# A graph convolution on one core: in steps 0 to 3, a chunk's message is made ahead of the last sum of a later pair's softplus on VectorE

## The chip, the core and the metric

The kernel runs on one core of one Trainium2 chip. Its time is the device time of one execution in microseconds (us), and of several runs the median. Engines are named as in the profile: PE (TensorE, matmuls), PEld (its weight loads), DVE (VectorE), ACT (ScalarE), POOL (GpSimd) and SP (SyncE, which here only issues DMAs). Each engine goes through its own queue in order; they wait for each other through semaphores.

## What is computed

A layer of a SchNet-like graph network with a residual: 12500 nodes with 128 features, 412500 directed edges with 20 radial features and a weight each. Shortened from the reference:

```python
h = jnp.maximum(_layernorm(x, axis=-1), 0.0)
def ssp(x): return jax.nn.softplus(x) - LOG2
h = h @ W_in2f
Wij = ssp(f_ij @ W_f1 + b_f1) @ W_f2 + b_f2      # per edge, 128 filters
Wij = Wij * rcut_ij[:, None]
x_ij = h[idx_j] * Wij                            # idx_j = dst (sorted)
agg = jax.ops.segment_sum(x_ij, idx_i, num_segments=N)   # idx_i = src
return x + ssp(agg @ W_o1 + b_o1) @ W_o2 + b_o2
```

## The kernel before

Edges are taken in order, in 806 chunks of 512 (four tiles of 128 edges); four chunks make a group, which shares its input loads. A chunk goes through these parts, each a method of `Group`:

- `rows` (L608): SP fetches the 32 rows of h near the chunk's destinations into `near`, as three bf16 parts. `window` (L744): DVE compares the destinations, relative to the chunk's first (`rel`, loaded by SP at L593), with row numbers, which gives a selection matrix `at`.
- `hidden`, `hidden_log`, `hidden_end`, for a pair of chunks together (1024 edges): PE makes z = f W_f1 (L653) in a PSUM buffer of which there is one; ACT takes the absolute value and the exponential (L656, L657), then the logarithm (L662); DVE adds the rest of the softplus, r = max(z, -b) + a (L668). That is "the last sum of a pair's softplus".
- `bias` (L753 for chunks 0 and 1, else L757 on ACT) puts the second bias into a PSUM buffer v; `value` (L764) adds r W_f2 to it on PE; `pick` (L772) selects h's rows with `at` and `near` on PE, and `picked` (L780) scales them by the edge weight on ACT into `hg`, in four instructions.
- `message` (L789, L791, L795): for the first chunk of a pair DVE copies the places of its edges into `o`; then DVE multiplies v by hg into `o`, and POOL scatters the four tiles to `slots`, a table in DRAM, each row to a slot of its own near the other edges of its source node.
- `blocks`, `rank`, `rank_end` (L673, L692, L725, L697, L717 to L721) count the free slots: DVE marks the sources' blocks, PE adds the marks up in one PSUM buffer `free`, and DVE reduces and makes the slots' numbers.

The table has seven segments; when a segment's chunks are through, its units are loaded by SP (L833), compared (L844) and added up by matmuls (L857), beside the chunks of the segments after it. Clears of the tables go out on SP (L1099) by a plan of due times. After the last chunk the last segment is added up and the output part is made.

The order of work is written out by hand. `step(k)` runs for k from -1 on, and each call puts instructions on the queues of all engines, for several chunks at different depths: `part(name, upto, make)` makes a part for all chunks that are due and not made yet. The part "end" is made up to chunk min(k + 2, the last one with a logarithm), and `pairs` lets it do something only for the first chunk of a pair; so it does something in steps of even k. The part "window" is made up to k + 2, and at k = 0 up to 1. The message of a step is that of chunk k; its value and pick are those of chunk k + 1, and its bias that of chunk k + 2. The buffers that matter: three for `r`, three for `at`, four for `o`, two for `hg`, three in PSUM for v and the picked rows together, one for z.

In the first steps normalisation and projection of h (`make_h`) stand between the parts, a piece after each step.

Of the kernel before, what the change touches and what calls it, by code (L numbers as in the profile page):

```python
# [41 lines left out]
def gnn_kernel(  # L42
# [475 lines left out]
    with tc.tile_pool(name="edge", bufs=2) as edge, tc.tile_pool(  # L518
# [367 lines left out]
        LG, LW, LR, LZ = 12, 6, 6, 4  # L886

        def of(k):
            return groups[k // NCHUNK], k % NCHUNK
# [6 lines left out]
        made = {}  # L896

        def part(name, upto, make):

            for j in range(made.get(name, -1) + 1, min(upto, NCH - 1) + 1):  # L900
                make(*of(j))
                made[name] = j

        def pairs(make):
            return lambda g, c: None if c % 2 else make(g, c)
# [22 lines left out]
        def group(j):  # L928
            if j not in groups and j < NG:
                groups[j] = Group(j)  # L930

        def ranks(j):

            if 0 <= j < NCH:
                g, c = of(j)
                g.rank(c)
                yield
                g.rank_end(c)

        def step(k, units=()):  # L940

            def has(j):
                return 0 <= j < NCH

            group((k + LG) // NCHUNK)
            part("rows", min(k + LW, 2 * k + 3, NEXT if k < NEXT - 3 else NCH), rows)
            for c, u in units:
                c.load(u + AHEAD)  # L950

            part("blocks", min(k + LR + 1, 2 * k + 1), blocks)
            part("end", min(k + LZ - 2, made.get("log", -1)), pairs(hidden_end))
            part("window", k + 2 if k > 0 else k + 1, window)
            if has(k):
                g, c = of(k)
                g.message(c, vs.pop(k), hgs.pop(k))
            for c in owed:
                c.keep()
            owed.clear()  # L960
            if has(k + 1):
                g, c = of(k + 1)
                vs[k + 1] = g.value(c, bs.pop(k + 1))
                ps = psum.tile([P, QT, P], F32, name="picked", tag="v", bufs=3)
                g.pick(c, ats.pop(k + 1), ps)
            if has(k + 2):

                bs[k + 2] = of(k + 2)[0].bias(of(k + 2)[1])
            if has(k + 1):
                hgs[k + 1] = g.picked(c, ps)  # L970
            for c, u in units:
                c.compare(u)
            upto = max(made["rank"], min(k + LR, 2 * k + 1))
            ready = [ranks(j) for j in range(made["rank"] + 1, upto + 1)]
            made["rank"] = upto
            for r in ready[:1]:
                next(r, None)
            part("hidden", k + LZ, pairs(hidden))
            part("log", k + LZ - 1, pairs(hidden_log))
            for c, u in units:  # L980
                if summed:
                    summed[0].add(summed[1])
                summed[:] = c, u
            for r in ready:
                for _ in r:
                    pass
# [21 lines left out]
        end = NCH + 6  # L1008
        rate = {}
        while len(rate) < len(at):  # L1010
# [4 lines left out]
            end = at[j]  # L1015
# [9 lines left out]
        i, k = 0, todo[0][0]  # L1025
# [43 lines left out]
        with tc.manual_schedule():  # L1069
# [27 lines left out]
            for k in range(-1, max(NCH, max(units) + 1)):  # L1097
                for seg, d in zeros.get(k, ()):
                    seg.clears.append(nc.sync.dma_start(*d).ins.name)  # L1099
                now = units.get(k, ())  # L1100
                for c, u in now:
                    if u == 0:
                        for i in range(AHEAD):
                            c.load(i)
                step(k, now)

                for m in h:
                    next(m, None)
                if k > NEXT - 3:
                    next(aside, None)  # L1110
# [101 lines left out]
```

## Time and profile before

| what | value |
|---|---|
| median of three runs | 5770.01 us (5732.79, 5770.01, 5771.6) |
| the profiled execution, own time | 5772.48 us |
| its span, first to last instruction | 5770.8 us |
| mean granted TensorE clock | 0.718 |
| busy: PE, PEld, DVE, ACT, POOL | 3877.3, 2912.2, 3382.9, 2715.3, 3103.5 us |
| scatters of POOL (L795) | 3224, of 962 ns each |
| sums of the softplus on DVE (L668) | 403, of 1281 ns each |
| products on DVE (L791) | 806, of 680 ns each |
| first scatter starts | 29.44 us |

In the profile's groups a row reads: line, engine, operation, tile written <- tiles read, shapes, count | busy us, mean ns of one | idle time of the engine just before them and what ended it. In the timeline a row begins with start and duration in us, and the bracket at its end is the idle time ahead of it and its releaser. "remote" is an event that the profile puts down to none of the core's engines; "issue" means that nothing that the profile shows was waited for.

### The profile page before, as it was taken

What the parts mean: (1) busy time and instruction counts of PE and PEld (TensorE: products, weight loads), DVE (VectorE), ACT (ScalarE), POOL (GpSimd) and SP (SyncE); (2) the same over time, 40 slices, a digit from 0 to 9 for tenths busy, and PEclk for the clock granted to TensorE, in tenths of its full rate; (3) what the DMA queues carried; (4) which work ended last, traced back from release to release, by engine and by line L of the source; (5) the groups of instructions that cost most, each with busy time, mean ns of one, the idle gap of its engine ahead of it and who ended that gap; (6) DMA issues with size and microseconds to landing.
All of it is one profiled execution on the core that took longest, in us unless ns stands there. A gap on an engine that the chain in (4) does not pass through costs nothing. (4 is left out here: it accounts for less than half of the span.)

```text
span 5770.8 us, 71871 instructions
## 1 busy us (share of the span) xinstructions
PE 3877.3 (67%) x21576; PEld 2912.2 (50%) x21576; DVE 3382.9 (59%) x6726; ACT 2715.3 (47%) x5490; POOL 3103.5 (54%) x3244
## 2 busy tenths in 40 slices
PE   5556555556555555577777777777777777777778
PEld 3333333333333333356655666566566665655557
DVE  5555555555444444466665666666666666566767
ACT  4455554555444444444444444444444444444444
POOL 5555555555555555555555555555555555555550
PEclk7665566565556566578777787788877788787879
DMA  5444443343333333255664554655555555555547
GB/s 150 138 135 141 130 141 119 115 137 104 99 89 87 106 109 87 82 152 161 188 183 137 158 160 144 190 163 157 160 168 173 154 150 178 165 141 153 145 126 215
DMA packets 515581, 820.80 MB, mean 142 GB/s; under 512 B 177074, under 2 KB 312870, under 8 KB 515186
## 3 DMA queue, kind: packets, MB, share of 16 engines
q1 hardware_dynamic: 411586, 602.85, 37.4%
q0 software_dynamic: 103168, 213.15, 11.2%
q8 instruction: 176, 2.88, 0.2%
q14 instruction: 219, 1.79, 0.1%
q10 hardware_dynamic: 432, 0.13, 0.0%
HBM read 419.09 MB, written 396.64 MB: 141 GB/s over the span
## 5 line engine op out<-in xcount | busy, mean ns | idle before, releaser
L795 POOL DMA_INDIRECT slots<-o,slot x3224 | 3100.3, 962 | 2522.6 <-DVE o L791 1605.2
L764 PE MATMUL v<-wf,r 128*128 128x128 f32 x6448 | 1209.4, 345 | 527.4 <-ACT a L657 207.3
L857 PEld LDWEIGHTS acc<-to,m 128*128 128x128 f32 x8132 | 1249.1, 238 | 577.1 <-issue 280.8
L857 PE MATMUL acc<-to,m 128*128 128x128 f32 x8132 | 1342.0, 329 | 271.0 <-DVE agg L880 136.4
L764 PEld LDWEIGHTS v<-wf,r 128*128 128x128 f32 x6448 | 1077.6, 251 | 850.7 <-issue 301.8
L780 ACT ACTIVATE hg<-picked,rcut 128x128 f32<-128x128 f32 x3224 | 913.1, 365 | 1256.6 <-remote 801.2
L697 DVE TENSOR_REDUCE top<-free 128x4 f32<-128x392 f32 x806 | 451.5, 560 | 1650.5 <-remote 990.2
L757 ACT ACTIVATE v<-bf 128x512 f32<-128x512 f32 x804 | 478.0, 595 | 1212.9 <-DVE o L791 888.5
L653 PE MATMUL z<-f,wf 20*128 20x512 f32 x1612 | 661.1, 881 | 406.9 <-DVE r L668 242.4
L844 DVE TENSOR_TENSOR to<-count_ps,m 128x512 f32<-128x512 f32 (+3 forms) x824 | 644.7, 806 | 255.3 <-remote 109.3
L772 PE MATMUL picked<-near,at 96*128 96x128 bf16 x3224 | 398.5, 257 | 495.3 <-ACT hg L780 317.4
L668 DVE SCALAR_TENSOR_TENSOR r<-z,nbf,a 128x1024 f32<-128x1024 f32 x403 | 516.2, 1281 | 242.3 <-ACT a L662 136.3
L656 ACT ACTIVATE a<-z,bf 128x1024 f32<-128x1024 f32 x403 | 454.0, 1127 | 400.4 <-remote 267.8
L772 PEld LDWEIGHTS <-at 96*128 96x128 bf16 x3224 | 315.5, 118 | 558.1 <-issue 531.3
L791 DVE TENSOR_TENSOR o<-v,hg 128x512 f32<-128x512 f32 x806 | 547.8, 680 | 16.8 <-ACT hg L780 12.8
L744 DVE TENSOR_TENSOR at<-count_ps,rel 96x512 bf16<-96x512 f32 x806 | 545.3, 677 | 0.0
L653 PEld LDWEIGHTS z<-f,wf 20*128 20x128 f32 x1612 | 174.6, 241 | 620.9 <-issue 428.9
L662 ACT ACTIVATE a<-a,half 128x1024 f32<-128x1024 f32 x403 | 468.1, 1162 | 0.0
L673 DVE TENSOR_TENSOR inb<-count_ps,blk 128x392 f16<-128x392 f32 x806 | 445.9, 554 | 0.0
L657 ACT ACTIVATE a<-a 128x1024 f32<-128x1024 f32 x403 | 425.8, 1057 | 12.8
L725 PE MATMUL free<-inb,rest_of 128*128 128x392 f16 x806 | 335.3, 416 | 117.6 <-issue 46.9
L692 PE MATMUL free<-inb,after 128*128 128x392 f16 x806 | 335.9, 417 | 17.4 <-issue 13.6
(108 smaller groups left out, 1142.5 us busy)
## 6 DMA issues: line engine op xcount, KB each, us to landing
m<-slots SPq DMA_DIRECT2D x311, 387.0 KB
m<-slots SPq DMA_DIRECT2D x317, 258.0 KB
rel<-rel_d SPq DMA_DIRECT2D x202, 384.0 KB
m<-slots SPq DMA_DIRECT2D x172, 322.5 KB
slots<-o,slot POOLq DMA_INDIRECT x3224
slots<-zero SPq DMA_DIRECT2D x96, 387.0 KB
slots<-zero SPq DMA_DIRECT2D x64, 516.0 KB
f<-in_f_t SPq DMA_DIRECT2D x404, 80.0 KB
```

Source lines behind the costliest of these rows:

```text
L653: nc.tensor.matmul(z[:, k, :], wf1[rows, :], self.f[rows, :], start=True, stop=True)
L662: nc.scalar.activation(a, a, AF.Ln, bias=half, scale=0.5)
L668: nc.vector.scalar_tensor_tensor(r, z, nbf1, a, op0=ALU.max, op1=ALU.add)
L744: nc.vector.tensor_tensor(at, prow_ps.to_broadcast([WP, CH]), self.rel[:, c, :], op=ALU.is_equal)
L757: nc.scalar.activation(v, spread(bf12, QT), AF.Copy)
L764: nc.tensor.matmul(v[:, i, :], r[:, i * P:(i + 1) * P], wf2, start=False, stop=True, skip_group_check=True)
L772: nc.tensor.matmul(ps[:, i, :], at[:, i * P:(i + 1) * P], near, start=i == 0, stop=i == QT - 1, skip_group_check=True)
L780: nc.scalar.activation(hg[:, i, :], ps[:, i, :], AF.Copy, scale=self.rcut[:, j:j + 1])
L791: nc.vector.tensor_mul(o[:, :, :P], v, hg)
L795: put = nc.gpsimd.indirect_dma_start(out=views[j % VIEWS], out_offset=bass.IndirectOffsetOnAxis(ap=self.slot[:, j:j + 1], axis=0), in_=o[: ...
L844: nc.vector.tensor_tensor(to[:, :n, :], count_ps[:, None, :].to_broadcast([P, n, P]), self.m[u][:, :n, P:].to_broadcast([P, n, P]), op=ALU ...
L857: nc.tensor.matmul(self.acc[b // QT][:, i, :], m[:, j, :P], to[:, j, :], start=t == 0, stop=t == self.seg.tiles(b) - 1)
```

## The change

In steps with k < 4 the part "end" is made after the message of the step, and not ahead of the part "window"; from step 4 on the order is as before.

```diff
             part("blocks", min(k + LR + 1, 2 * k + 1), blocks)
-            part("end", min(k + LZ - 2, made.get("log", -1)), pairs(hidden_end))
+            early_on = k < 4
+
+            def end():
+                part("end", min(k + LZ - 2, made.get("log", -1)), pairs(hidden_end))
+
+            if not early_on:
+                end()
             part("window", k + 2 if k > 0 else k + 1, window)
             if has(k):
                 g, c = of(k)
                 g.message(c, vs.pop(k), hgs.pop(k))
+            if early_on:
+                end()
             for c in owed:
                 c.keep()
```

## The prediction

> **What bounds the kernel now.** I read the page first, for the span and the load of each engine, then the view of waits for the whole span, then the timeline of the first 60 us, since the edit acts only there.
>
> The page:
>
> ```profile
> span 5770.8 us, 71871 instructions
> PE 3877.3 (67%) x21576; PEld 2912.2 (50%) x21576; DVE 3382.9 (59%) x6726; ACT 2715.3 (47%) x5490; POOL 3103.5 (54%) x3244
> L795 POOL DMA_INDIRECT slots<-o,slot x3224 | 3100.3, 962 | 2522.6 <-DVE o L791 1605.2
> ```
>
> No engine is full: PE, the busiest, is busy for 67%. The kernel is a pipeline whose steps wait for one another: 806 messages of four scatters each (3224), and POOL, which sends them, idles 2522.6 us, mostly for DVE's product (L791).
>
> The view of waits:
>
> ```profile
> POOL slots L795 <- DVE o L791: 1605.2, 358, 25.4
> DVE top L697 <- remote: 990.2, 163, 12.1
> ACT v L757 <- DVE o L791: 888.5, 325, 9.0
> ```
>
> The columns are us in total, times, and the longest. DVE stops longest at the reduction L697, which needs the ranking matmuls; those stand on PE behind the matmuls that need the rows of `near` fetched by SP. ACT refills a PSUM buffer (L757) only when L791 has read it. So a step is a ring DVE - ACT - PE - DVE with DMA arrivals in it. What the edit can win for good is a shift of this ring at the start; nothing makes a later step shorter.
>
> The timeline, DVE alone, around steps 0 and 2 (start, duration, instruction, idle time before it and its releaser):
>
> ```profile
> 19.61 0.53 DVE L673 TENSOR_TENSOR inb<-count_ps,blk 128x392 f16<-128x392 f32 x1
> 26.60 1.28 DVE L668 SCALAR_TENSOR_TENSOR r<-z,nbf,a 128x1024 f32<-128x1024 f32 x1 [6.46 <-ACT a L662]
> 27.80 0.68 DVE L744 TENSOR_TENSOR at<-count_ps,rel 96x512 bf16<-96x512 f32 x1
> 28.47 0.68 DVE L791 TENSOR_TENSOR o<-v,hg 128x512 f32<-128x512 f32 x1
> 29.83 0.57 DVE L697 TENSOR_REDUCE top<-free 128x4 f32<-128x392 f32 x1 [0.68 <-PE free L692]
> ...
> 39.07 1.27 DVE L668 SCALAR_TENSOR_TENSOR r<-z,nbf,a 128x1024 f32<-128x1024 f32 x1
> 40.26 0.68 DVE L744 TENSOR_TENSOR at<-count_ps,rel 96x512 bf16<-96x512 f32 x1
> 40.86 0.16 DVE L789 COPY o<-place 128x8 f32<-128x8 f32 x1
> 40.93 0.68 DVE L791 TENSOR_TENSOR o<-v,hg 128x512 f32<-128x512 f32 x1
> 41.53 0.55 DVE L697 TENSOR_REDUCE top<-free 128x4 f32<-128x392 f32 x1
> ```
>
> In step 0, DVE stands idle for 6.46 us at the sum L668 (pair 2, 3), until ACT's logarithm ends, with message 0 behind it. In step 2 the same sum (pair 4, 5) waits for nothing: DVE goes through it back to back.
>
> PE, and the DMA engines while this happens (timeline, then the table by stretches, whose last columns are granted clock, DMA share, GB/s):
>
> ```profile
> 28.54 0.61 PE L772 MATMUL picked<-near,at 96*128 96x128 bf16 x4 [3.45 <-DVE at L744]
> 34.28 0.61 PE L772 MATMUL picked<-near,at 96*128 96x128 bf16 x4 [0.47 <-issue]
> 40.58 1.46 PE L653 MATMUL z<-f,wf 20*128 20x512 f32 x4
> ```
> ```profile
> 25.00:29.00 4.00, 0.55 (x6) 0.47 (x6) 2.40 (x4) 1.93 (x4) 0.00 (x0) 1.00 1.02 312
> ```
>
> The pick of chunk 1 waited for `at`, which stood behind the sum. In 25 to 29 us the DMA engines have no room (share 1.02, 312 GB/s).
>
> **The change, part by part.** It adds no work. It moves one part past another in steps 0 to 3, but the sum is made only for the first chunk of a pair and a fixed distance ahead, so in steps 1 and 3 there is none to move. Two places change, all on DVE's queue: steps 0 and 2. There `at`, the copy of places and the product come ahead of the sum. The orders of PE, ACT, POOL and SP stay; what they wait for comes at other times.
>
> Step 0. `at` needs only `rel`, so it follows L673 at 20.1 us instead of 27.80. The product then needs ACT's L780 for chunk 0 (four, started 21.10, 1.14 us in all, so 22.24): it runs at about 22.3 instead of 28.47, 6.2 us earlier. POOL starts 0.97 us after the product starts (28.47 to 29.44), so the first scatter goes at about 23.2 instead of 29.44. Behind the product now waits the sum, but it had to wait for ACT until 26.57 anyway; the cover is 26.6 - 22.9 = 3.7 us, and the sum keeps its 26.60.
>
> What is late next. After the sum DVE reaches L697 at 27.8 instead of 29.83, if the ranking matmuls are done: PE's pick of chunk 1 can follow the values that end at about 25.1 (started 23.01, 2.08 us), so yes. DVE leads by 29.83 - 27.80 = 2.0 us through step 1. PE has one buffer for z: L653 for pair 4, started 29.73 before, now waits for the sum's end at 27.9, about 1.6 to 1.8 us earlier. Then the pick of chunk 2 needs its `near`. The 256-byte packets, which these fetches alone use, ran for chunks 2 and 3 from 30.31 to 32.6 us in the trace, landing at 32.9. The pick stood at 34.28, so its lead can be at most 34.28 - 32.95 = 1.33 us. And message 0's four scatters, 4 x 128 rows x 516 B = 264 KB, started packets at 31.16 and now start them some 6 us sooner, into the full stretch: at 312 GB/s that is 0.85 us by which `near` lands later. Ends: lead 1.33 us (scatters find gaps) and 0.48 us (none). The row of 1.02 stands nearer to the second, so I take 0.48.
>
> A rule speaks against the early scatters from another side. The 1.12 us of four tensor-scalar instructions on DVE (L344, from 31.57) ran beside scatters started 30.88, 32.14 and 33.41, each 0.96 us with 0.30 us between, as elsewhere: nothing was held up. The Trainium skill, SBUF — State Buffer, section Who interferes with whom, says that copies and tensor-scalar instructions of DVE can take a port pair shared with GpSimd for their whole length, so that the other blocks. By it the moved copy (0.16 us) could hold one scatter of message 1 for 0.16 us; by the row it holds none, and POOL has idle time after it in either case, so the sum stays the same.
>
> Step 2. Nothing is waited for, so this is only an exchange: the product goes 40.26 - 39.07 = 1.19 us earlier, and the sum goes 41.53 - 40.26 = 1.27 us later. Waiting for the sum is z of the next pair (L653 at 40.58, 0.24 us after the sum's end at 40.34), and behind z on PE stand the ranking matmuls of chunk 4, which hold DVE at 42.66. Earlier is ACT's refill (L757 at 41.64), which had 3.00 us of idle time and is followed by L780 and then L656, which needs that same z. So the sum sets the end, and the early product only idles ACT elsewhere.
>
> Sum: lead out of step 1, -0.48; exchange in step 2, +1.27; together +0.8 us (ends: -1.33 + 1.27 = -0.1 where the scatters find gaps, -2.0 + 1.27 = -0.7 where `near` didn't bind at all, +1.27 where step 1 keeps no lead). From step 4 on the program is as before, and the ring runs from a start moved by this. The profiled execution took 5772.48 us (span 5770.8 and 1.7 around it), 2.5 above the median of the three runs, 5770.01; against it the sum gives 5773.3, against the median 5770.8. Only 0.01% is at stake, and the runs shown spread over 5732.79 to 5771.6, 0.7%.
>
> **The rivals.**
> *The lead lives on.* If the ranking of chunk 4 follows the early product and not z, the 2.0 us of step 1, or even the 6.2 of message 0, stay: 5770.0 - 2.0 = 5768.0, at best 5763.8. For it: POOL's 25.45 us of idle time before its first scatter is the longest of its waits. Against it: POOL idles 1.33 us again at its next message, so its start sets nothing.
>
> *The moved phase makes more waits (slower).* The ring and the DMA traffic of clears, `rel` and `near` meet at other moments; a fetch that lands late stops DVE for 990.2 / 163 = 6.1 us. Four more such waits give 5770.0 + 24 = 5794; from ten more (+61 us) the change is slower by over 1%. For it: 163 such waits in 806 chunks say that the margin is thin. Against it: the same program meets such shifts in each run, and they stay within 0.7%.
>
> *The moved phase makes fewer waits.* Six less give 5770.0 - 37 = 5733, which is where one of the runs of before already stands.
>
> **How the numbers follow.** Forecast, a shift of -0.7 to +1.3 us on a run like the median: 0.60, own range 5763 to 5778, and 5770.8 its value. Lead lives on: 0.10. More waits: 0.15, of which 0.04 over 1%. Fewer: 0.15, of which 0.03 over 1%. About 1% is what a measurement of this kernel tells from no change; the runs shown spread by 0.7%. So faster by over 1% 0.03, within 1% 0.93, slower 0.04. The range reaches to the other cases: down to 5728, just under the run at 5732.79, and up to 5798, past four more waits.
>
> **What would show it.** Right: the first scatter at about 23 us; the sum of step 0 still near 26.6 and now the last of its group; DVE's L697 after it near 27.8; the sum of step 2 at 39.9 (39.07 - 0.48 + 1.27); scatters from message 3 on within 1.5 us of their old times; later stretches with the same step length. Wrong: the sum of step 0 later than 26.6 (the product waited for something else), a lead of 2 us or more at 100 us, or a step length that differs by over 1% between 100 and 2440 us, where before has 1378 scatters.

## The result and the profile after

| | kernel before | changed kernel |
|---|---|---|
| median of 20 runs each, us | 5742.41 (5704.52 to 5783.67) | 5750.82 (5729.53 to 5769.17) |
| profiled execution, us | 5772.48 | 5740.27 (span 5738.6) |

(The table's runs are called the first executions below.) The ratio of the times is 1.0009, with a 95% interval from 0.9993 to 1.0025: 5 us more, between 4 less and 14 more (the medians themselves differ by 8.4 us). That is no change that can be measured, as forecast. The forecast of 5770.8 us stands 20 us above the median of 5750.82 us, which lies below the forecast's own range of 5763 to 5778 us and only inside the wider one, 5728 to 5798, that takes in the rivals. The profiled execution of the changed kernel is 32 us shorter than that of before; the twenty runs of each say that this is not the edit.

The page of the changed kernel has the same loads:

```profile
span 5738.6 us, 71872 instructions
PE 3856.3 (67%) x21576; PEld 2897.2 (50%) x21576; DVE 3377.4 (59%) x6726; ACT 2715.8 (47%) x5490; POOL 3096.3 (54%) x3244
L795 POOL DMA_INDIRECT slots<-o,slot x3224 | 3093.1, 959 | 2501.4 <-DVE o L791 1589.3
```

Its view of waits (us in total, times, longest):

```profile
POOL slots L795 <- DVE o L791: 1589.3, 366, 19.3
...
ACT v L757 <- DVE o L791: 866.6, 324, 9.3
DVE top L697 <- remote: 830.9, 136, 11.7
```

The longest wait of POOL for a product fell from 25.4 to 19.3 us: that is message 0, 6.1 us earlier. The totals moved by far more than the 6 us that the edit gives (DVE at L697 from 990.2 to 830.9), which the section on the pauses below explains.

The edit itself is seen in the timeline of DVE of the changed kernel:

```profile
20.24 0.68 DVE L744 TENSOR_TENSOR at<-count_ps,rel 96x512 bf16<-96x512 f32 x1
...
22.32 0.69 DVE L791 TENSOR_TENSOR o<-v,hg 128x512 f32<-128x512 f32 x1 [1.32 <-ACT hg L780]
26.64 1.28 DVE L668 SCALAR_TENSOR_TENSOR r<-z,nbf,a 128x1024 f32<-128x1024 f32 x1 [3.63 <-PE free L692]
27.84 0.56 DVE L697 TENSOR_REDUCE top<-free 128x4 f32<-128x392 f32 x1
...
36.49 0.57 DVE L697 TENSOR_REDUCE top<-free 128x4 f32<-128x392 f32 x1 [3.09 <-PE free L692]
...
40.65 0.68 DVE L791 TENSOR_TENSOR o<-v,hg 128x512 f32<-128x512 f32 x1
41.25 1.27 DVE L668 SCALAR_TENSOR_TENSOR r<-z,nbf,a 128x1024 f32<-128x1024 f32 x1
```

Step 0 went as worked out: `at` at 20.24, the product at 22.32, the sum still at 26.64, L697 at 27.84 and not 29.83, so DVE leads by 2.0 us. In step 2 the sum stands behind the product, but it starts at 41.25, not at the 39.9 forecast. What came between is on PE, in the timeline of the changed kernel:

```profile
27.98 1.13 PE L653 MATMUL z<-f,wf 20*128 20x512 f32 x4 [1.78 <-issue]
...
35.22 0.58 PE L772 MATMUL picked<-near,at 96*128 96x128 bf16 x4 [4.63 <-DMA near<-h]
...
42.66 1.48 PE L653 MATMUL z<-f,wf 20*128 20x512 f32 x4 [1.84 <-DVE r L668]
```

z of the pair starts 1.75 us earlier (27.98, before 29.73). Then the pick of chunk 2 waits 4.63 us for the DMA of `near` and starts at 35.22, where it started at 34.28 before: the lead of 2.0 us has become 0.94 us of delay. The exchange in step 2 adds 1.1 us, so that z of the next pair starts 2.08 us late (42.66, before 40.58). The clock granted to PE differs as well: the tables by stretches (us, busy time of PE, PEld, DVE, ACT, POOL, granted clock, DMA share, GB/s), first of before, then of the changed kernel,

```profile
42.00:46.00 4.00, 2.88 (x26) 2.52 (x25) 2.78 (x6) 3.97 (x9) 3.08 (x4) 1.00 0.59 152
```
```profile
42.00:46.00 4.00, 3.33 (x13) 2.08 (x14) 2.04 (x5) 2.81 (x6) 3.09 (x4) 0.66 0.29 73
```

show 13 matmuls in place of 26 at a clock of 0.66 in place of 1.00. That need not be the edit's doing: the kernel before, run again below ("same"), has 0.57 in these 4 us.

From here on I follow the edit by the start of the first scatter of each message, changed kernel less kernel before, since a total hides a shift of a few us:

| message | 0 | 1 | 2 | 3 | 4 | 6 | 8 | 10 | 12 | 50 | 300 | 500 | 750 |
|---|---|---|---|---|---|---|---|---|---|---|---|---|---|
| us | -6.1 | -2.0 | -0.3 | +1.0 | +1.7 | -0.9 | +5.9 | -2.7 | +5.2 | -6.3 | -3.1 | +0.8 | -28.3 |

Up to message 4 this is the edit, together with what one execution of the same kernel differs from the next there (+0.9 to +3.0 at message 4, below). Then the difference jumps up and down, by some 6 us between neighbouring messages at the larger jumps, and reaches nearly 30 us later.

### The profile page after: what moved, and what is told of

It is laid out like the page before. It is cut to its first block, busy times and chain, and to the rows that moved or that the text cites. A ratio compares the mean times of both kernels' runs of the same rounds, so it can differ in the third digit from the quotient of the medians.

```text
span 5738.6 us, 71872 instructions
## 1 busy us (share of the span) xinstructions
PE 3856.3 (67%) x21576; PEld 2897.2 (50%) x21576; DVE 3377.4 (59%) x6726; ACT 2715.8 (47%) x5490; POOL 3096.3 (54%) x3244
## 5 line engine op out<-in xcount | busy, mean ns | idle before, releaser
L780 ACT ACTIVATE hg<-picked,rcut 128x128 f32<-128x128 f32 x3224 | 913.2, 365 | 1318.0 <-remote 827.2
L857 PEld LDWEIGHTS acc<-to,m 128*128 128x128 f32 x8132 | 1236.2, 236 | 595.4 <-issue 315.4
L697 DVE TENSOR_REDUCE top<-free 128x4 f32<-128x392 f32 x806 | 450.8, 559 | 1596.8 <-remote 830.9
```

The lines of the kernel that those rows point to most:

```text
L780: nc.scalar.activation(hg[:, i, :], ps[:, i, :], AF.Copy, scale=self.rcut[:, j:j + 1])
L857: nc.tensor.matmul(self.acc[b // QT][:, i, :], m[:, j, :P], to[:, j, :], start=t == 0, stop=t == self.seg.tiles(b) - 1)
```

## Where the wander comes from: pauses

The prediction put the 990.2 us of "remote" waits at L697 down to fetches of `near` that land late. The timeline of before at one of them says otherwise:

```profile
397.90 0.02 SPq L608 DMA_DIRECT2D near<-h  x1
...
398.19 0.33 PE L692 MATMUL free<-inb,after 128*128 128x392 f16 x1
...
402.05 1.16 PE L764 MATMUL v<-wf,r 128*128 128x128 f32 x8
...
408.55 1.14 ACT L780 ACTIVATE hg<-picked,rcut 128x128 f32<-128x128 f32 x4 [6.55 <-remote]
409.27 0.57 DVE L697 TENSOR_REDUCE top<-free 128x4 f32<-128x392 f32 x1 [7.91 <-remote]
```

The ranking matmul that L697 reads starts at 398.19 and is short, and the packets of `near` had run by 398.09; yet DVE starts L697 only at 409.27 and ACT its L780 at 408.55. The records of PE's semaphore have no update from 396 us on until five stand at 408.52 to 409.46. These records have gaps (3100 of PE's 3663 updates are there), but all waits of this kind agree: each of the 163 "remote" waits at L697 and of the 152 at L780 in this trace ends within 0.1 us after an update of PE's, and the matmul waited for had started 7.9 and 9.2 us earlier in the median. So what is late there is what PE signals, not a fetch. Stretches in which PE, DVE and ACT all idle for more than 3 us: 73 in this trace (337 us), 81 in that of the changed kernel (386 us). The waits at L697 come one in 35 us in the mean. Of the 245 messages of this trace that follow the one before by more than 7.5 us, 189 have a "remote" wait of over 1.5 us in the step, of the 392 that follow within 5.3 us only 22: where such waits fall in two traces makes most of the wander.

## The experiments

Two theories stood. **A**, the prediction's: the edit is a shift of a few us made in the first steps, carried from there unchanged, and all later differences are the wander of waits that either kernel has. **The rivals**: the edit does something that lasts (it makes or removes waits in later steps, or the early product helps or hurts at each message), or a shift at the start is lost on the way. Message offsets below are against the run "same"; runs start up to 0.4 us apart, so offsets in the first messages are good to that; by message 700 two executions have drifted apart by up to 3 us more. Each offset is from one profiled execution.

The experiments ran on two chips (the last three on the second), on which the kernel before took 4235.95 us (6 runs; one more run, beside the first four experiments, took 4227.57) and 4238.22 us (23 runs), not 5742 us. On which chip the first executions ran is not known. So first the kernels themselves.

### same: the kernel before, unchanged

> The kernel before, unchanged. Theory A (the edit acts in the first 50 us only; what differs later is chance in how DMA arrivals meet the steps): against the first execution of before, the first six messages' scatters start within 0.3 us, and from message 20 on the difference wanders by 5 to 30 us with no trend. Theory B (the first 50 us themselves differ by chance from run to run): messages 1 to 4 differ by 1 us or more, as they did between before and after.

4247.9 us, above the six runs of this kernel (4230.0 to 4238.9). Its first five messages agree with the first profiled execution within 0.3 us, then it gains steadily, 76 us by message 50 and 1509 by the last. Page and waits:

```profile
span 4246.2 us, 71871 instructions
PE 3403.7 (80%) x21576; PEld 2608.9 (61%) x21576; DVE 3374.3 (79%) x6726; ACT 2682.7 (63%) x5490; POOL 3101.1 (73%) x3244
L795 POOL DMA_INDIRECT slots<-o,slot x3224 | 3098.0, 961 | 1016.3 <-issue 795.4
```
```profile
ACT v L757 <- DVE o L791: 1384.0, 473, 8.2
POOL slots L795 <- issue: 795.4, 2608, 0.6
...
PE z L653 <- DVE r L668: 318.1, 305, 5.7
...
POOL slots L795 <- DVE o L791: 53.0, 65, 25.7
```

The instructions are the same, and so is their work on DVE (3374.3 us, before 3382.9), ACT and POOL; PE is busy for 3403.7 us in place of 3877.3, at a mean granted clock of 0.819 in place of 0.718. No row of its waits says "remote", and there is not one stretch over 3 us in which PE, DVE and ACT all idle. POOL waits for products 53.0 us in place of 1605.2, and its idle time ahead of the scatters, 1016.3 us in place of 2522.6, is shorter by 1506 us, nearly the whole difference of the spans (1525 us). Its timeline shows what paces the kernel here:

```profile
102.83 0.96 POOL L795 DMA_INDIRECT slots<-o,slot  x1 [0.30 <-issue]
104.09 0.96 POOL L795 DMA_INDIRECT slots<-o,slot  x1 [0.30 <-issue]
105.36 0.96 POOL L795 DMA_INDIRECT slots<-o,slot  x1 [0.31 <-issue]
```

Scatters follow one another with 0.30 us between; two take 2.53 us (102.83 to 105.36), so the four of a chunk 5.06. A chunk takes 5.08 us (mean of messages 30 to 300), 6.75 us in the first executions. POOL is the bound there, which the prediction did not have. For the experiments this is a gift: without wander the edit's shift in the first messages can be read to 0.4 us.

### again: the changed kernel, unchanged

> The changed kernel, unchanged. A: message 0 about 6.1 us earlier than before, message 1 about 2.0 earlier, message 4 again 1.5 to 2 later, the pick of chunk 2 at 34.5 to 35.7 us (35.22 in the first execution). B: the pick of chunk 2 anywhere from 33 to 36, message 4 from -1 to +2.

4243.98 us. Offsets: -6.3, -2.1, -0.5, +1.4 for messages 0 to 3, +3.0 for message 4, and then nearly constant (+3.0 at 50, +4.3 at 700; -0.3 at the last, since "same" loses some 4.6 us in its last 100 messages). What is decided by message 4 stays, as theory A has it, and POOL shows why: ahead of a message's first scatter it idles for more than the usual 0.30 us at messages 1, 2, 3, 4 and 6 and then no more; in "same" at 1, 2, 4 and 6 and then not before message 738. In the first execution of the kernel before it does so ahead of 413 of the 805 messages behind the first. So the carrying is shown where POOL always has the next scatter at hand; in the first executions the wander hides whether a shift of a few us is carried.

```profile
34.93 0.59 PE L772 MATMUL picked<-near,at 96*128 96x128 bf16 x4 [2.71 <-DMA near<-h]
...
42.38 2.06 PE L653 MATMUL z<-f,wf 20*128 20x512 f32 x4 [2.12 <-DVE r L668]
```

Again the pick of chunk 2 waits for `near`, and z for the sum.

### step0 and step2: one half of the change each

```diff
-            early_on = k < 4
+            early_on = k < 2
```

> Step 0 alone moved (k < 2), step 2 as before. A: messages 0 and 1 at -6.1 and -2.0 us against before, the pick of chunk 2 again near 35.2 (late fetch), and in step 2 the sum at 40.0 in place of 41.25, its product at 41.9; message 4 at +0.2 to +0.8, so 1.2 less than with both steps moved. If the exchange in step 2 costs nothing: message 4 at +1.7, as with both.

4234.82 us. Message 0 at -6.2, message 1 at -2.1, and from message 2 to 700 a constant +0.3: nothing is left of the 2 us, nor lost. The pick of chunk 2 starts at 34.57, in "same" at 34.55; first "step0", then "same":

```profile
34.57 0.58 PE L772 MATMUL picked<-near,at 96*128 96x128 bf16 x4 [2.32 <-DMA near<-h]
```
```profile
34.55 0.61 PE L772 MATMUL picked<-near,at 96*128 96x128 bf16 x4 [0.47 <-DVE at L744]
```

```diff
-            early_on = k < 4
+            early_on = k == 2
```

> Step 2 alone moved (k == 2), step 0 as before. A: messages 0 and 1 as before within 0.3 us, message 2 1.2 earlier, the sum of step 2 1.27 later at 40.3, z after it at 41.8 and messages 3 and 4 1.0 to 1.4 us later than before. If the exchange costs nothing: message 4 within 0.3 of before.

4239.22 us. The sum goes to 40.21 and z to 41.62, 1.20 us later than in "same" (40.42), as the exchange says. Yet message 6 and those behind it stand at -0.1 up to message 100 (-0.8 at 700). What may give the 1.2 us back is seen on PE and in the granted clock, first "step2", then "same":

```profile
41.62 1.13 PE L653 MATMUL z<-f,wf 20*128 20x512 f32 x4 [1.10 <-DVE r L668]
43.92 1.06 PE L764 MATMUL v<-wf,r 128*128 128x128 f32 x8
```
```profile
44.02 1.91 PE L764 MATMUL v<-wf,r 128*128 128x128 f32 x8
```
```profile
42.00:46.00 4.00, 3.53 (x28) 2.47 (x25) 2.77 (x6) 2.70 (x4) 2.75 (x3) 1.00 0.51 139
```
```profile
42.00:46.00 4.00, 3.93 (x22) 3.80 (x22) 2.72 (x6) 3.97 (x9) 3.08 (x4) 0.57 0.68 199
```

The eight matmuls of the values of chunk 4 take 1.06 us at a clock of 1.00 and 1.91 us at 0.57; z starts 1.2 us later, and the values end earlier. The two halves give +0.3 and -0.1 alone, and +3.0 together in "again". They do not add up (though one kernel alone differs by 2 us from execution to execution, see "both_timed"), and the clock's rows differ; in "again" they read

```profile
42.00:46.00 4.00, 3.62 (x11) 1.98 (x12) 1.47 (x4) 2.23 (x5) 3.08 (x4) 0.55 0.20 59
46.00:50.00 4.00, 3.54 (x19) 3.07 (x18) 2.36 (x5) 2.79 (x7) 1.54 (x3) 0.59 0.67 198
```

That the clock is the cause is a reading of these rows; it was not tried by itself and is not shown.

The Trainium skill, TensorE: Matmul & The Clock Gate, section What's actually happening, has PE at half rate after an idle window of about 3.4 us, at full rate after as long a busy one, and no rate between. On the rates the traces agree: their clock records hold 1.0 and 0.5 alone (the values of the rows above are means), and 1.06 and 1.91 us fit the two. On the times "again" does not: its clock goes to 0.5 at 42.44 us after PE had waited only 2.12 us, and stays there for 6.83 us, in all of which PE shows as busy. So here the records, not the rule, say when PE is slow and for how long.

### window0: without the early scatters

In steps 0 and 1 the sum is made between `at` and the message, so `at` is early and the product, with its scatters, is not.

```diff
+            early_on = k < 2
...
             part("window", k + 2 if k > 0 else k + 1, window)
+            if early_on:
+                end()
             if has(k):
                 g, c = of(k)
                 g.message(c, vs.pop(k), hgs.pop(k))
```

> In step 0 only the selection matrix (window) goes ahead of the sum; the message stays behind the sum, so its scatters start near 28.8 us and not 23.3. Theory A (message 0's early scatters make the fetches of near late): the pick of chunk 2 at 33.0 to 33.8 us, against 35.22 with the early scatters and 34.28 before; message 1 1.3 us earlier than before, messages 2 to 4 about 1.0 earlier. Theory B (near is late for another reason, such as the other DMAs, which stay): the pick of chunk 2 at 34.8 or later.

4231.87 us. The product goes at 28.04, and the pick of chunk 2 at 33.50, 1.07 us earlier than in "step0":

```profile
33.50 0.58 PE L772 MATMUL picked<-near,at 96*128 96x128 bf16 x4 [1.31 <-DMA near<-h]
```

Messages 6 to 32 stand at -1.5 (-4.4 at 700). So without the early scatters of message 0 `near` lands 1.07 us earlier, in this pair of executions; the forecast had 0.85. All executions together are in the next section.

### step0_late_clears: the clears out of the way

"step0", with the plan of the clears begun at step 8.

```diff
-        t0, i = 0, 0
+        t0, i = 8, 0
```

> Step 0 alone moved, and the first clears of the table on SP's queue begin 8 steps later, which takes some 0.4 MB per clear out of the full stretch at 25 to 37 us; their due times stay. A: near for chunk 2 has landed by 33, the pick of chunk 2 stands at 32.3 to 33.0 us right behind its selection matrix, messages 1 to 4 are 1.5 to 2.2 us earlier than before, and at message 50 the lead is lost in the wander of several us. B (the stretch is full without the clears too): the pick of chunk 2 at 34.5 or later.

4248.09 us. Here "step0", then this kernel:

```profile
29.00:33.00 4.00, 3.25 (x12) 1.78 (x8) 3.88 (x14) 2.17 (x2) 0.00 (x0) 1.00 1.03 318
```
```profile
29.00:33.00 4.00, 1.30 (x10) 0.97 (x8) 3.89 (x14) 2.17 (x2) 0.00 (x0) 0.62 0.69 205
```

(The clock's 1.00 in the first row is no measurement: the clock's records of "step0" begin at 39.37 us, and its eight matmuls of values took 2.08 us at 30.17, in this kernel 1.24 at 29.05.) The DMA share is down from 1.03 to 0.69, and the pick goes at 33.11, 1.46 us earlier than in "step0":

```profile
33.11 0.59 PE L772 MATMUL picked<-near,at 96*128 96x128 bf16 x4 [2.82 <-DMA near<-h]
```

It still waits 2.82 us for `near`. Messages 6 to 20 stand at -2.5. So the lead of step 0 was worth 2.5 us at most; the time saved at the start does not reach the end: from -4.7 at message 700 the offset goes to +1.8 at 738 and ends at -0.7.

In this pair the 1.46 us are not faster transfers but an earlier issue. A clear also takes its turn on SP's queue ahead of the fetch (1.32 us to issue in "step0", at 25.11). Here SP issues the fetch of `near` for chunk 2 1.43 us earlier than in "step0", and from issue to landing (the last record of the fetch's semaphore) it takes 5.56 us, in "step0" 5.58. Issue and landing of this fetch in all executions in which the start was not delayed, in us:

| kernels | issued by SP | landed |
|---|---|---|
| early scatters (first execution after, "again", "step0", "all_steps", "both_timed") | 28.92, 28.16, 28.85, 28.53, 28.47 | 35.08, 34.79, 34.43, 34.44, 34.20 |
| no early scatters (first execution before, "same", "step2", "window0") | 29.18, 29.18, 27.70, 28.05 | 32.88, 33.34, 32.96, 33.36 |
| early scatters, late clears ("step0_late_clears", "both_late_clears") | 27.42, 28.21 | 32.98, 33.21 |
| neither ("window0_late_clears") | 27.62 | 31.65 |

(Of the landing at 32.88 only 3 of 16 records are in the trace.) The landings do not overlap between rows that differ in one thing: the early scatters make `near` land 1.45 us later in the mean, and the clears do about as much (1.49 us), in part because SP issues the fetch later. Executions that do the same up to there spread by 1.5 us in the issue and 0.9 us in the landing, so 1.07 and 1.46 are values of single pairs.

The Trainium skill, DMA: Bandwidth & Descriptors, section Issuing engines are not separate DMA queues, says that what POOL and SP start runs on the same 16 engines and interleaves. The first two rows agree: POOL's scatters hold SP's fetch, although SP issues it no later.

### all_steps: the exchange in every step

```diff
-            early_on = k < 4
+            early_on = True
```

> The same exchange in every step of even k, 403 times. If the sum sets the path wherever PE waited for it to make z (186 times in before) at 1.27 us each: 236 us slower, +4%, and at most 403 x 1.27 = 512 us, +9%. If the product sets it (ACT's refill and POOL wait for it, 325 and 358 times, half of them at even k) at 1.19 us each: about 200 us faster, -3.5%. If neither, because DMA arrivals set the step: within 1%.

4275.33 us (4 runs), 1.0099 of the time before (1.0063 to 1.0135), 1% slower. Offsets are +1.3 at message 4, then +1.8 to +3.8 up to message 600; between 600 and 650 (3075 to 3344 us, beside the adding up of segments) 15.7 us come on, and +21.3 at the last. So each theory that priced the exchange at every chunk, for good or ill, fell, for a kernel that POOL paces; with the pauses it was not tried. The waits show why:

```profile
POOL slots L795 <- issue: 789.8, 2590, 0.6
ACT v L757 <- DVE o L791: 777.3, 485, 6.6
...
PE z L653 <- DVE r L668: 711.1, 335, 8.2
```

PE's wait for the sum grows from 318.1 to 711.1 us and ACT's for the product falls from 1384.0 to 777.3; POOL's steps stay at 5.07 us per chunk (messages 30 to 300), since POOL sets the pace. This trace has 14 stretches over 3 us in which PE, DVE and ACT all idle (55 us, none of them a "remote" wait), all before 1600 us, and they leave the offset where it was. In the stretch from 600 to 650 POOL does run out of products, ahead of eight messages from 625 on, for 1.7 to 3.6 us; why was not followed.

### delay60: a late start and nothing else

56 fills of an unused tile on DVE ahead of step 0.

```diff
+                if k == 0:
+                    for _ in range(56):
+                        nc.vector.memset(idle, 0.0)
```

> The kernel before with 56 fills of an unused 128 x 1024 tile on DVE ahead of step 0, about 60 us in which DVE can do nothing else. Theory A (a shift at the start is carried to the end, one for one): the total rises by the length that the fills take in the trace, 60 us, within the 10 us that the runs scatter. Rival (the start is covered by later work, or SP's queue uses the pause to get ahead): less than half of it, under 30 us.

4296.76 us (4 runs), ratio 1.0144 (1.0126 to 1.0162): 53 to 69 us more. Offsets: +59.8 at message 0, +58.6 at 50, +57.1 at 700 and +52.4 at the last ("same" loses some 4.6 us at its end). A late start is carried nearly one for one where POOL paces the kernel; no slack on the way takes it in. That settles the rival of the lost shift for these executions: the 2 us of step 0 are lost where the trace shows it, at message 2, not by and by.

### both_timed, both_late_clears, window0_late_clears

The changed kernel once more, timed against the kernel before:

> The changed kernel, timed against the kernel before on this chip, where runs of before lay within 4230.0 to 4238.9 us. In the second execution of the changed kernel every message from 4 to 700 stood 3.0 to 4.4 us behind before. If that offset is the edit's own (the state of the start carried to the end): the median 2 to 5 us above that of before, +0.05 to +0.12%, and the offset at message 50 again +2.5 to +3.5. If it was chance of one execution: a median within 2 us of before, and the offset at message 50 between -1 and +1.

4239.46 us (12 runs, before 4238.22 of 23), ratio 1.0007 (0.9998 to 1.0015): 0.8 us less to 6.4 more. In its profiled execution message 4 stands at +0.9 and message 50 at +0.7, where "again" had +3.0; the granted clock of 42 to 46 us was 0.69, of the next 4 us 0.88 (in "again" 0.55 and 0.59). By message 700 it is at -1.3. So one and the same kernel sets out with +0.9 or +3.0: the offset of "again" was chance of one execution.

The changed kernel with the clears begun at step 8, as above:

> Both steps moved as in the change, with the first clears 8 steps later. If the two moves simply add (step 0 with late clears left -2.5 us, step 2 alone -0.1): message 50 at -2.6 against before. If the exchange of step 2 costs its 1.27 us: -1.2. If the 3 us of the change come from the PE running at half clock after the long wait for the late fetch (granted clock 0.55 to 0.59 in 42 to 50 us, where step 2 alone had 1.00): the wait is gone here, the clock in 42 to 46 us is 1.00 again and message 50 stands at -2.6 to -1.2, not at +3.

4245.59 us. The pick of chunk 2 goes at 33.35, messages 6 to 32 stand at -1.1, the clock of 42 to 46 us is 1.00. Beside the -2.5 of "step0_late_clears" the exchange of step 2 costs 1.4 us here, one execution of each. With the clears out of the way the sign of the change's start turns; by the last message it stands at +1.1.

"window0" with late clears, the best start of both, timed:

> In step 0 only the selection matrix goes ahead of the sum, the message stays behind it, and the first clears go out 8 steps later: neither early scatters nor clears in the stretch in which near is fetched. Message 50 at -2.0 to -3.0 us against before; the median 1 to 4 us below that of before, 0.1% at most. If the clears begun later cost waits later on: no gain or a loss of several us at the end.

4244.01 us (11 runs), ratio 1.0011 (1.0000 to 1.0023). Offsets: -2.2 at message 50, -3.2 at 600, then it loses 2 us before message 640 and 7 from 700 to 770, and ends at +5.0. A version that beats both kernels was not found.

## Why the prediction was right and wrong

- *Only steps 0 and 2 change; step 0 by 6.2 us.* Right: product at 22.32 (22.3), first scatter 6.1 us earlier, sum at 26.64, L697 at 27.84.
- *`near` of chunk 2 eats the lead.* The mechanism was right, and this step of the sum failed by its size: the 0.85 us by which the early scatters make `near` land later. It measured 2.20 us in the first executions (landing at 32.88 before, 35.08 after), 1.45 us in the mean between the rows of all executions. So "lead out of step 1, -0.48" became +0.94 in the first executions and 0.0 in "step0". The 0.85 counted the scatters' bytes at 312 GB/s behind the old landing at 32.95; it did not ask in which order transfers already queued would go, nor how far the issue on SP's queue moves from one execution to the next (27.70 to 29.18 us for the kernel before and "step2", which do the same up to there).
- *Exchange in step 2, +1.27.* Measured 1.2 us at z ("step2"), so sized right. "The sum sets the end" was not the whole of it: at message 6 nothing of it was left in "step2", 1.4 us in "both_late_clears", more in "again". The rows of PE's granted clock, which the forecast left out, differ there; that they are the cause is not shown.
- *Sum +0.8 us (-0.7 to +1.3).* At message 4, +1.7 (first executions), +3.0 ("again"), +0.9 ("both_timed"): the sign is right, the upper end too low in two of three; as one kernel sets out with +0.9 or +3.0 and by message 700 with -1.3 or +4.3, that the sum came near +0.8 is luck. In the times, +5 us (-4 to +14) and +1.2 (-0.8 to +6.4): not to be told from nothing.
- *The ring runs from a shifted start.* The outcome was right in the experiments: offsets stay nearly constant from message 7 to 700 ("step0" +0.3 at both, "again" +3.1 and +4.3), and "delay60" is carried. The mechanism was another: POOL's unbroken scatters carry the shift there, not a ring of waits. In the first executions, on which the forecast was made, neither is shown.
- *The level, "against the median 5770.8".* This is the step that failed in the number. The sum stood on 5770.01 us, the median of three runs; the median of twenty is 5742.41, 27.6 us lower, and the runs spread over 79 us. With that level the sum would have given 5743.2, 7.6 us below the measured 5750.82. The own range of 5763 to 5778 was 15 us wide although the three runs at hand, 5732.79 to 5771.6, spread over 39: the shown spread went into the wide range and not into the value or its own range.
- *A fetch that lands late stops DVE for 6.1 us.* Wrong: all 163 of these waits end with a late update of PE's. Where they are absent, POOL is the bound, with 5.06 of 5.08 us per chunk.
- *Rivals.* The lead did not live on. More or fewer waits for good were not seen: without pauses the offset stays within 3 us for 700 messages, and with them it wanders in either direction.

Open: what the pauses are. Both profiled executions of the first set have them; on the two chips of the experiments no wait at L697 or L780 is "remote", and stretches over 3 us are few (none in "same" and "step2", one to three in the others, 14 in "all_steps"). No edit was tried that could switch them on or off, and whether the chip makes the difference was not tried. The stretches over 3 us add up to 337 us of the some 1500 us between the two levels; PE's lower clock goes with them, and whether it is a cause or follows from the waits is not known.

## What to carry to other kernels

A head start that is made at one engine is worth what the next late thing leaves of it: here a fetch, held by the scatters that the head start itself sent earlier, took all of the 2 us. Judge an edit of a few us by where each message or chunk starts in the trace, not by totals that spread by 1%; look at more than one execution; and take the level from many runs, or forecast against the spread. Where one engine always has work at hand, as POOL here, a shift at the start is carried to the end nearly one for one, so it can be no larger than what the first steps show.

## What was not expected of the hardware

- The same program took 5742 us in one set of runs and 4236 to 4238 us on two other occasions, with the same instructions and equal busy time of DVE, ACT and POOL within 1.5%; PE was busy for 3877 us in place of 3404. In the longer executions PE's updates come late at 163 waits of DVE (6.1 us in the mean) and 152 of ACT (5.3 us), in the shorter ones at none.
- PE's granted clock in one and the same stretch (42 to 46 us) was 0.55 to 0.69 in five executions and 1.00 in others, also for the same kernel (1.00 and 0.57 before the change); eight matmuls took 1.91 or 1.06 us there, as much as an edit of 1 us.
- Four tile scatters cost POOL 5.06 us per chunk (0.96 us each and 0.30 to the next, 1.26 to 1.27 us in the median of every trace here), which is the floor of this kernel's step.
- The first clear, which SP only issues, took 1.17 to 1.82 us of SP's queue, and the fetch of `near` stands behind it.
